# Layer 1's row terms by way of VectorE and DRAM, and a new pace for the dense jobs at the end, in a two-layer graph-attention kernel on Trainium2

## The chip, the cores and the metric

One core of a Trainium2 chip runs the whole program. The metric is the device time of one execution in microseconds (us). TensorE is called PE (matmuls) and PEld (its weight loads), VectorE DVE, ScalarE ACT, GpSimd POOL, and SyncE SP. SP does no arithmetic here: it issues most of the DMA transfers, in the order in which the program lists them. POOL issues the indirect transfers (gathers and scatters of rows by an index).

## The reference, cut to what matters

The input is 64 batches of 256 nodes with 256 features, all in float32, and one adjacency matrix. There are two layers, each a graph attention followed by a feed-forward part, with a layernorm before each and a residual behind each. Layer 0 has four heads and a dense feed-forward. Layer 1 is the one that the change touches:

```python
h = jnp.matmul(inp, W)                       # inp = layernorm(x)
e_src = jnp.einsum('bnf,f->bn', h, a1)
e_dst = jnp.einsum('bnf,f->bn', h, a2)
e = leaky_relu(e_src[:, :, None] + e_dst[:, None, :], 0.01)
attention = softmax(where(adj == 0, -1e9, e))
x = x + relu(matmul(attention, h))
# then, for every token, the two best of 8 experts:
h = gelu(tokens @ w1[e] + b1[e]); y = h @ w2[e] + b2[e]
out = out + combine[:, e:e + 1] * y
```

The score matrix `e` needs one term along the rows and one along the columns. The kernel holds one of them per partition. The other has to appear along the free dimension, the same in all 128 partitions: these are the "row terms" of the title.

## The kernel before, in words

**Steps and ranks.** The whole program is put in order by a planner at the end of the kernel (L1240 to L1282). Each job is a Python generator. A batch begins every three steps (`TICKS = 3`). In a step the planner resumes all active jobs in the order of their rank. `yield 45` ends a job's part of this step and gives its rank in the next one; `yield -26` asks to be resumed within the same step, at rank 26. So the order of instructions on every engine and on every DMA queue is the order of steps and ranks.

**One batch** (`batch_layers`) goes through some 20 steps. Of layer 0: rank 22 projects (L469), rank 24 scales on DVE (L485) and turns the four heads' row terms with a 32x32 block transpose into `ut` (L537). Rank 31 of the same step writes `ut` to a scratch tensor in DRAM (L621), rank 52 reads it back into all 128 partitions of `z` (L554, 512 KB). These two transfers are on SP's queue from batch 18 on (`SETTLED` is 18). The scores (L570) follow two steps later and read the terms from `z` itself.

Of layer 1: twelve steps after the batch's start `projected1` runs at rank 20. PE multiplies (L504), and ACT makes the exponentials `ex` (L511), the scaled `q` (L512) and the mask times one term, `me` (L517). One step later, at rank 25, `scores1` (L520) lets PE transpose the column `ex[:, t, 1:2]`, repeated over 128 columns, into the PSUM tile `pd` (L523, two transposes per batch). DVE then makes the scores `z1` from `pd` (L528, two instructions per batch). One step later, at rank 40, `attended` multiplies them with `q` (L584).

Because a batch starts every three steps, layer 1's `projected1` of batch b shares its step with layer 0's projection of batch b + 3.

**Experts.** The first 61 batches (`ROUTED`) are routed: POOL sends every token's row to its two experts' regions in DRAM (L1066), and whole pairs of 128-row tiles are worked on by `expert_pair`. It loads rows and weights (L906, L917, L935), turns the rows (L117), and some steps later runs `hidden` (L968 and the gelu L974), then `result` (L983, L993) and the weighting (L961). Then `scatter` adds the two tiles to the output with two indirect transfers (L1004). Each of the two waits for both transfers of the pair before. There are 129 pairs. From step 165 on (`SINGLE_AT`) at most one pair begins per step. The tile `y` that a scatter reads has nine buffers.

The last three batches are not routed. Each of 8 experts is applied to all their rows (`dense_expert`: L968, L983, L1036): a first group of batch 61 alone, and a second of batches 62 and 63. These sixteen jobs wait in `dense_jobs` and are begun by the planner. The next one begins once as many steps have gone by as the last one has batches:

```python
            if dense_jobs and step >= dense_free:
                units, job = dense_jobs.pop(0)
                dense_free = step + units
                begin(job(), 90)
```

Of the kernel before, what the change touches and what calls it, by code (L numbers as in the profile page):

```python
# [9 lines left out]
F32 = mybir.dt.float32  # L10
I32 = mybir.dt.int32
AF = mybir.ActivationFunctionType
ALU = mybir.AluOpType
AX = mybir.AxisListType

P = 128
# [5 lines left out]
def rows_to_all(ap: bass.AP, n: int) -> bass.AP:  # L22

    return bass.AP(tensor=ap.tensor, offset=ap.offset, ap=[[0, P], [1, n]])
# [3 lines left out]
def kernel(  # L28
# [17 lines left out]
    nc = tc.nc  # L46
    B, N, D = x.shape
# [4 lines left out]
    NT = N // P  # L52
# [21 lines left out]
    work = ctx.enter_context(tc.tile_pool(name="work", bufs=2))  # L74
    small = ctx.enter_context(tc.tile_pool(name="small", bufs=4))
# [3 lines left out]
    def bank(name, shape):  # L79
        t = psum.tile([P, 2 * D], F32, tag="bank", name=name, bufs=8)  # L80
        n = 1
        for s in shape:
            n *= s
        t = t[:, :n]
        if len(shape) == 2:
            t = t.rearrange("p (a b) -> p a b", a=shape[0])
        elif len(shape) == 3:
            t = t.rearrange("p (a b c) -> p a b c", a=shape[0], b=shape[1])
        return t
# [22 lines left out]
    S = 32  # L112
    G = P // S
# [15 lines left out]
    SETTLED = CHUNKS[0] + CHUNKS[1] + CHUNKS[2] + CHUNKS[3] + 2  # L129


    ident = const.tile([P, P], F32, tag="ident", name="ident")
# [186 lines left out]
    def once(work):  # L319
# [14 lines left out]
        out=tri, in_=tri, pattern=[[1, P]], base=0, channel_multiplier=-1,  # L334
# [64 lines left out]
    def finish_norms(n):  # L399
        mv, rstd = half_done.pop()  # L400
        if at_end():
            var = small.tile([P, 2 * NT], F32, tag="sq", name="var", bufs=4)[:, :n]
            nc.vector.tensor_scalar(var, mv[:, :n, 1], EPS, None, op0=ALU.add)
            inverse_root(rstd[:, :n], var)
            return
        nc.gpsimd.tensor_scalar_add(rstd[:, :n], mv[:, :n, 1], EPS)  # L406
        nc.gpsimd.tensor_tensor(rstd[:, :n], rstd[:, :n], mhalf[:, :n], ALU.pow)
# [84 lines left out]
    for i in range(2):  # L492
        t = keep.tile([P, NT, D + 1], F32, tag=f"q1_{i}", name=f"q1_{i}")
# [3 lines left out]
    def projected1(xT, rstd, b):  # L497

        q = q1s[b % 2]
        pqs = []  # L500
        for t in range(NT):
            pq = bank("pq", [D + 3])
            for k in range(KT):
                nc.tensor.matmul(  # L504
                    pq, xT[:, k, t * P : (t + 1) * P], wx1[:, k, :],
                    start=(k == 0), stop=(k == KT - 1),
                )
            pqs.append(pq)
        ex = small.tile([P, NT, 3], F32, tag="ex1", name="ex1")
        for t, pq in enumerate(pqs):  # L510
            nc.scalar.activation(ex[:, t, :], pq[:, D:], AF.Exp, scale=rstd[:, t : t + 1])  # L511
            nc.scalar.activation(  # L512
                q[:, t, :D], pq[:, :D], AF.Copy, scale=rstd[:, t : t + 1]
            )
        me = work.tile([P, NT, N], F32, tag="me", name="me", bufs=1)
        for j in range(NT):
            nc.scalar.activation(me[:, j, :], masks[1][:, j, :], AF.Copy, scale=ex[:, j, 0:1])  # L517
        return q, ex, me

    def scores1(ex, me):  # L520
        pd = bank("pd", [N])
        for t in range(NT):
            nc.tensor.transpose(  # L523
                pd[:, t * P : (t + 1) * P], ex[:, t, 1:2].to_broadcast([P, P]), ident
            )
        z = work.tile([P, NT, N], F32, tag="z1", name="z1", bufs=1)
        for j in range(NT):
            nc.vector.scalar_tensor_tensor(  # L528
                z[:, j, :], pd, ex[:, j, 2:3], me[:, j, :], op0=ALU.max, op1=ALU.mult
            )  # L530
        return [z[:, j, :] for j in range(NT)]

    def send_terms(q, b):


        ut = small.tile([P, S], F32, tag="ut", name="ut", bufs=1)
        nc.vector.transpose(  # L537
            ut.rearrange("p (t h w) -> p t h w", t=NT, h=H), q[:, :, :, HD - 1 : HD + 3]
        )
        ud = tc.dram_tile([S, S], F32, name=f"terms_{b}")  # L540
        ud = ud.rearrange("c r -> (c r)").rearrange("(c p) -> c p", p=P)
        return ut, ud
# [51 lines left out]
    def batch_layers(b, c0, xng, lg):  # L594
# [23 lines left out]
        if b:  # L618
            ut, ud = send_terms(q, b)
            yield -31  # L620
            terms_queue(b).dma_start(  # L621
                out=ud.rearrange("c (g r) -> g c r", g=G),
                in_=ut[2 : P : S // (NT * H), :],
            )
            yield -52
        z = work.tile([P, NT, NT, H, P], F32, tag="z4", name="z4", bufs=2)
# [17 lines left out]
        ex = work.tile([P, NT, D], F32, tag="e", name="e", bufs=1)  # L644
# [21 lines left out]
        for t in range(NT):  # L666
            nc.vector.scalar_tensor_tensor(  # L667
                x2[:, t, :], pf[:, t, :], rstd[:, t : t + 1], x1b[:, t, :],
                op0=ALU.mult, op1=ALU.add, accum_out=sums[:, t : t + 1],
# [6 lines left out]
        xT = transposed(x2)  # L676
        yield 20
        q, ex, me = projected1(xT, rstd, b)
        yield 25
        z = scores1(ex, me)  # L680
        yield 40
        pvs, rinv = attended(
            q[:, :, None, :], 1, lambda j, h, t: z[j][:, t * P : (t + 1) * P]
# [9 lines left out]
        for t in range(NT):  # L693
            nc.vector.scalar_tensor_tensor(
                x2[:, t, :], x2[:, t, :], 1.0, rel[:, t, :],
                op0=ALU.mult, op1=ALU.add, accum_out=sums[:, t : t + 1],
# [36 lines left out]
        if not dense:  # L733
            d = nc.sync.dma_start(
                out=out_rows[b * N : (b + 1) * N, :].rearrange("(t p) d -> p t d", p=P), in_=base
# [262 lines left out]
    def scatter():  # L998

        y, xt = scatters.pop(0)  # L1000
        before = added[-2:] + based
        based.clear()
        for t in range(2):
            d = nc.gpsimd.indirect_dma_start(  # L1004
                out=out_rows, out_offset=bass.IndirectOffsetOnAxis(
                    ap=xt[:, t, 0:1].bitcast(I32), axis=0
                ),
                in_=y[:, t, :], in_offset=None, compute_op=ALU.add,
            )
            nc.gpsimd.nop()  # L1010
            tc.declare_no_dep(
                d.ins, query=SYNC, group="out", keep=before,
                reason="the rows of a pair are all different",
            )
            for ins in before:
                tc.add_manual_dep(d.ins, ins.name, AFTER, reason="added to before")
            tc.add_to_no_dep_group("out", d.ins)
            added.append(d.ins)
# [37 lines left out]
    active = []  # L1056
    waiting, dense_jobs = [], []
    sent = []

    def begin(job, rank):  # L1060
        active.append([rank, len(order), job])
        order.append(job)
# [172 lines left out]
    step, more, credit = 2, True, 0.0  # L1235


    SETUP_AT = 4
    dense_free = 0
    with tc.manual_schedule():  # L1240
        while more or active or waiting or dense_jobs or scatters:
            phase = step % TICKS
            if more and (phase == 0 or step == 2):
                nxt = next(batches, None)
                more = nxt is not None
                if more:
                    begin(nxt, 40 if phase == 0 else 25)
            if step >= SETUP_AT and setup:
                begin(setup.pop(0)(), 90)
            if step >= SINGLE_AT:  # L1250
                if waiting and len(scatters) < 3:
                    begin(waiting.pop(0)(), 90)
            elif phase == 1:
                credit = min(credit + 3.0, 2.0)
                while waiting and credit >= 1.0:
                    credit -= 1.0
                    begin(waiting.pop(0)(), 90)
            if dense_jobs and step >= dense_free:
                units, job = dense_jobs.pop(0)
                dense_free = step + units  # L1260
                begin(job(), 90)
            if scatters:
                def one():
                    scatter()
                    return
                    yield
                begin(one(), 97)
            order_steps.append(step)
            queue = [(a[0], a[1], a) for a in active]
            heapq.heapify(queue)  # L1270
            while queue:
                *_, entry = heapq.heappop(queue)
                entry[0] = next(entry[2], None)
                if entry[0] is not None and entry[0] < 0:
                    entry[0] = -entry[0]
                    heapq.heappush(queue, (entry[0], entry[1], entry))
            if half_done:
                finish_norms(NT)
            if half_squared:
                finish_squares()  # L1280
            active[:] = [a for a in active if a[0] is not None]
            step += 1  # L1282
# [35 lines left out]
```

## Time and profile before

| | before |
|---|---|
| median of 3 runs | 1486.76 us (1486.30 to 1491.11) |
| profiled execution, its own time | 1489.83 us |
| span from first to last instruction | 1488.0 us |
| PE busy, PEld busy | 1420.1 us (95%), 1264.0 us (85%) |
| DVE busy | 1232.9 us (83%) |
| ACT busy | 1006.5 us (68%) |
| POOL busy | 864.6 us (58%) |
| moved by DMA | 236.10 MB, mean 159 GB/s |
| granted PE clock, mean | 0.985 |

The shares are averages over a start, a long middle in which two pairs and one batch are done every 20 us, a stretch from about 1050 us with one pair per step, and an end without batches from about 1310 us. A share of a stage is read from that stage alone. The ends of matmuls are modelled, so a busy PE is judged by the starts that follow each other and by the idle time ahead of them.

### The profile page before, as it was taken

How to read it: one execution, taken by the hardware profiler on the slowest of the kernel's cores; microseconds unless marked ns; L12 is line 12 of the kernel's file. 1: busy time of each engine (PE TensorE's matmuls, PEld its weight loads, DVE VectorE, ACT ScalarE, POOL GpSimd, SP SyncE). 2: the span in 40 equal slices, each digit the busy share in tenths (PEclk: the TensorE clock that was granted, in tenths of full speed). 3: DMA queues.
4: the chain of work that ended last, by engine and by line, in shares of the span. 5: the costliest groups of instructions: out<-in, count | busy, mean ns of one | idle time of the engine just before them, and what ended most of it. 6: DMA issues, size and time to landing. Idle time of an engine off the chain costs nothing. (4 is left out here: it accounts for less than half of the span.)

```text
span 1488.0 us, 29865 instructions
## 1 busy us (share of the span) xinstructions
PE 1420.1 (95%) x8138; PEld 1264.0 (85%) x8138; DVE 1232.9 (83%) x4320; ACT 1006.5 (68%) x2389; POOL 864.6 (58%) x851
## 2 busy tenths in 40 slices
PE   6899999999999999999999999999999999899994
PEld 5688888898999999899999989888888888778883
DVE  7689999988898889899888989998888888765442
ACT  1377667577777777777777787777777878643330
POOL 2122446455857676666758585776666668544444
PEclk9899999999999999999999999999999999999998
DMA  4832243567878777787877687768877786988743
GB/s 128 227 98 86 89 130 117 146 172 153 199 171 193 161 177 170 171 185 180 190 156 190 147 193 168 190 164 186 193 158 172 153 173 128 213 201 150 152 66 49
DMA packets 354081, 236.10 MB, mean 159 GB/s; under 512 B 246260, under 2 KB 316156, under 8 KB 353916
## 3 DMA queue, kind: packets, MB, share of 16 engines
q1 hardware_dynamic: 301000, 157.90, 42.1%
q0 software_dynamic: 48864, 66.33, 23.9%
q10 hardware_dynamic: 4052, 9.98, 2.3%
q8 instruction: 67, 1.10, 0.3%
q14 instruction: 98, 0.80, 0.2%
HBM read 146.00 MB, written 88.09 MB: 157 GB/s over the span
## 5 line engine op out<-in xcount | busy, mean ns | idle before, releaser
L1004 POOL DMA_INDIRECT out_dram<-y,xt x258 | 415.6, 1611 | 214.6 <-issue 54.6
L584 PE MATMUL pv<-q,z 128*128 128x65 f32 (+1 forms) x2560 | 363.7, 297 | 0.7 <-DVE z L570 0.3
L584 PEld LDWEIGHTS pv<-q,z 128*128 128x128 f32 x2560 | 331.2, 193 | 13.3 <-DVE z L570 1.3
L1066 POOL DMA_INDIRECT xs<-xng,pos x244 | 256.3, 1050 | 65.2 <-issue 57.7
L983 PE MATMUL py<-w2s,hT 128*128 (+1 forms) x1224 | 282.9, 382 | 4.7 <-ACT hT L974 4.5
L983 PEld LDWEIGHTS py<-w2s,hT 128*128 128x128 f32 x1224 | 229.7, 191 | 37.2 <-ACT hT L974 7.4
L570 DVE SCALAR_TENSOR_TENSOR z<-z,q,mask 128x256 f32<-128x256 f32 x504 | 231.5, 482 | 15.5 <-DMA z<-terms 6.5
L968 PE MATMUL ph<-sT,we 128*128 128x256 f32 x1032 | 241.4, 383 | 1.6 <-DVE sT L117 0.9
L968 PEld LDWEIGHTS ph<-sT,we 128*128 128x128 f32 x1032 | 195.6, 192 | 28.7 <-DVE sT L117 1.4
L961 ACT ACTIVATE y<-y,w 128x256 f32<-128x256 f32 x258 | 113.4, 499 | 119.4 <-DVE y L993 119.2
L459 ACT COPY xT<-pt 128x512 f32<-128x512 f32 x209 | 121.2, 588 | 82.1 <-PE pt L453 80.0
L974 ACT ACTIVATE hT<-ph,we 128x256 f32<-128x256 f32 x306 | 124.1, 472 | 64.1 <-PE ph L968 46.7
L406 POOL TENSOR_SCALAR rstd<-mv 128x4 f32<-128x4 f32 (+1 forms) x66 | 15.9, 240 | 224.8 <-DVE mv L379 175.3
L504 PE MATMUL pq<-wx,xT 128*128 128x259 f32 x512 | 126.5, 390 | 13.9 <-ACT xT L459 13.9
L424 ACT ACTIVATE off<-x,sums 128x256 f32<-128x256 f32 x256 | 129.2, 505 | 9.2 <-DVE x L667 3.3
L993 DVE TENSOR_TENSOR y<-py,b2s 128x512 f32<-128x512 f32 x129 | 86.9, 687 | 56.3 <-PE py L983 44.8
L469 PE MATMUL pq<-wx,xT 128*128 128x268 f32 x512 | 128.1, 394 | 2.4 <-DVE xT L117 1.2
L504 PEld LDWEIGHTS pq<-wx,xT 128*128 128x128 f32 x512 | 96.0, 192 | 33.6 <-ACT xT L459 19.8
L660 PE MATMUL pf<-wfT,xT 128*128 128x256 f32 x512 | 124.2, 386 | 0.0
L469 PEld LDWEIGHTS pq<-wx,xT 128*128 128x128 f32 x512 | 97.9, 192 | 21.7 <-DVE xT L117 1.4
L688 ACT ACTIVATE rel<-pv,rinv 128x256 f32<-128x256 f32 x128 | 54.0, 469 | 82.1 <-DVE rinv L591 81.8
L660 PEld LDWEIGHTS pf<-wfT,xT 128*128 128x128 f32 x512 | 94.9, 196 | 10.6
(170 smaller groups left out, 2355.7 us busy)
## 6 DMA issues: line engine op xcount, KB each, us to landing
we<-wpack SPq DMA_DIRECT2D x145, 288.0 KB
xr<-xs SPq DMA_DIRECT2D x516, 64.0 KB
z<-terms SPq DMA_DIRECT2D x46, 512.0 KB
xin<-in_x_dram SPq DMA_DIRECT2D x64, 256.0 KB
out_dram<-base SPq DMA_DIRECT2D x61, 256.0 KB
xblk<-in_x_dram SPq DMA_DIRECT2D x188, 64.0 KB
z<-terms ACTq DMA_DIRECT2D x17, 512.0 KB
out_dram<-y,xt POOLq DMA_INDIRECT x258
```

Source lines behind the costliest of these rows:

```text
L424: nc.scalar.activation(off, src[:, t, :], AF.Square, bias=sums[:, t : t + 1], scale=-float(D), accum_out=sq[:, at + t : at + t + 1],)
L459: nc.scalar.copy(dst, pt)
L469: nc.tensor.matmul(pq.rearrange("p h c -> p (h c)"), xT[:, k, t * P : (t + 1) * P], wx[:, k, :], start=(k == 0), stop=(k == KT - 1),)
L504: nc.tensor.matmul(pq, xT[:, k, t * P : (t + 1) * P], wx1[:, k, :], start=(k == 0), stop=(k == KT - 1),)
L570: nc.vector.scalar_tensor_tensor(z[:, j, :, h, :], terms, q[:, j, h, HD + 2 : HD + 3], masks[0][:, j, :].rearrange("p (t i) -> p t i", t=N ...
L584: nc.tensor.matmul(pv[:, h, :], z(j, h, t), q[:, j, h, : d + 1], start=(j == 0), stop=(j == NT - 1),)
L660: nc.tensor.matmul(pf[:, t, :], xT[:, k, t * P : (t + 1) * P], wfT[:, k, :], start=(k == 0), stop=(k == KT - 1),)
L968: nc.tensor.matmul(ph[:, f, :], we[:, k * D + f * P : k * D + (f + 1) * P], xT[:, k, :], start=(k == 0), stop=(k == KT - 1),)
L974: nc.scalar.activation(hT[:, f, :], ph[:, f, :], AF.Gelu, bias=we[:, C_B1 + f : C_B1 + f + 1])
L983: nc.tensor.matmul(py[:, t, :], hT[:, f, t * P : (t + 1) * P], w2s[:, e, f * D : (f + 1) * D].rearrange("p e c -> p (e c)"), start=(f == 0 ...
L1004: d = nc.gpsimd.indirect_dma_start(out=out_rows, out_offset=bass.IndirectOffsetOnAxis(ap=xt[:, t, 0:1].bitcast(I32), axis=0), in_=y[:, t, ...
L1066: d = nc.gpsimd.indirect_dma_start(out=xs_d[: E * CAP * PAIR, :], out_offset=bass.IndirectOffsetOnAxis(ap=at, axis=0), in_=xe, in_offset=None,
```

## The change

From batch 18 on, layer 1's row terms take the way that layer 0's terms take. In the step of `projected1`, at rank 26, DVE turns the column into `ut1` (`turned_terms1`). At rank 31 SP writes 256 floats to DRAM, and at rank 52 it reads them back into all 128 partitions of the second half of `z1` (128 KB). `scores1` then runs in the next step, as before, but at rank 45 instead of 25, and takes the terms from `z1` instead of `pd`. For the first 18 batches the transposes by PE stay.

The planner's `dense_free` becomes a fraction. As long as a pair waits or runs, a dense job is given 1.25 steps per batch of its group, and after that 0.5.

```diff
+    def turned_terms1(ex, b):
+        ut = small.tile([P, S], F32, tag="ut1", name="ut1", bufs=1)
+        nc.vector.transpose(
+            ut.rearrange("p (t w) -> p t w", t=NT),
+            ex[:, :, 1:2].to_broadcast([P, NT, S // NT]),
+        )
+        return ut, tc.dram_tile([N], F32, name=f"terms1_{b}")
+
+    def scores1(ex, me, z, spread):
+        terms = z[:, NT - 1, :]
+        if not spread:
+            terms = bank("pd", [N])
+            for t in range(NT):
+                nc.tensor.transpose(
+                    terms[:, t * P : (t + 1) * P], ex[:, t, 1:2].to_broadcast([P, P]), ident
+                )
         for j in range(NT):
             nc.vector.scalar_tensor_tensor(
-                z[:, j, :], pd, ex[:, j, 2:3], me[:, j, :], op0=ALU.max, op1=ALU.mult
+                z[:, j, :], terms, ex[:, j, 2:3], me[:, j, :], op0=ALU.max, op1=ALU.mult
             )
...
         q, ex, me = projected1(xT, rstd, b)
-        yield 25
-        z = scores1(ex, me)
+        spread = b >= SETTLED
+        if spread:
+            yield -26
+            ut, ud = turned_terms1(ex, b)
+            yield -31
+            nc.sync.dma_start(
+                out=ud.rearrange("(t g r) -> g t r", t=NT, g=G),
+                in_=ut[0 : P : S // NT, :],
+            )
+            yield -52
+        z = work.tile([P, NT, N], F32, tag="z1", name="z1", bufs=1)
+        if spread:
+            nc.sync.dma_start(out=z[:, NT - 1, :], in_=rows_to_all(ud, N))
+        yield 45 if spread else 25
+        z = scores1(ex, me, z, spread)
         yield 40
...
-    dense_free = 0
+    dense_free = 0.0
...
                 units, job = dense_jobs.pop(0)
-                dense_free = step + units
+                pairs = waiting or any(a[2].__name__ == "expert_pair" for a in active)
+                dense_free = max(dense_free, step - 0.5) + units * (1.25 if pairs else 0.5)
                 begin(job(), 90)
```

More of the change, by code (lines that the diff above doesn't have):

```diff
@@ L518, in projected1 @@
         return q, ex, me
[L520 to L526, printed above, removed]
+    def turned_terms1(ex, b):
[13 more added lines that the diff above has]
+                )
         for j in range(NT):
             nc.vector.scalar_tensor_tensor(
-                z[:, j, :], pd, ex[:, j, 2:3], me[:, j, :], op0=ALU.max, op1=ALU.mult
+                z[:, j, :], terms, ex[:, j, 2:3], me[:, j, :], op0=ALU.max, op1=ALU.mult
             )
```

## The prediction

> **What bounds the kernel now.** I read the stages first (busy time by windows), then the groups of instructions by shape, then the timeline of one step, then the waits of SP's queue, and last the timeline of the end. The first view has one row per stretch, with busy us and count for each engine.
>
> ```profile
> core 0: us, PE busy (x) PEld busy (x) DVE busy (x) ACT busy (x) POOL busy (x), PEclk, DMA share, GB/s
> 530.00:610.00 80.00, 80.00 (x478) 72.48 (x477) 71.49 (x245) 61.49 (x146) 54.58 (x52) 1.00 0.78 176
> 1050.00:1210.00 160.00, 155.74 (x879) 137.53 (x878) 137.57 (x487) 126.93 (x276) 108.39 (x98) 1.00 0.80 173
> 1310.00:1440.00 130.00, 127.70 (x594) 111.98 (x595) 69.76 (x187) 52.33 (x123) 57.78 (x38) 1.00 0.75 143
> ```
>
> From 370 to 930 us every stretch looks like the first row: four batches take exactly 80 us, and PE has no idle time at all. There, what PE no longer does is won, so long as nothing else comes to 20 us per batch. DVE is nearest: 71.5 of 80 us, some 3 us of small gaps between instructions, and 5.3 us of waiting (2.2 for ACT at L485, 1.9 for PE at L667, 1.1 at L993).
>
> The operations concerned, in the groups by shape (busy us, mean ns of one):
>
> ```profile
> L523 PE MATMUL pd<-ident,ex 128*128 128x128 f32 x128 | 26.2, 278 | 2.0 <-ACT ex L511 1.9
> L528 DVE SCALAR_TENSOR_TENSOR z<-pd,ex,me 128x256 f32<-128x256 f32 x128 | 53.8, 460 | 0.0
> L570 DVE SCALAR_TENSOR_TENSOR z<-z,q,mask 128x256 f32<-128x256 f32 x504 | 231.5, 482 | 15.5 <-DMA z<-terms 6.5
> L537 DVE STREAM_TRANSPOSE ut<-q 128x32 f32<-128x32 f32 x63 | 13.4, 212 | 2.2
> ```
>
> The 278 ns of a transpose is a latency. What it costs PE is the distance between starts:
>
> ```profile
> 810.93 0.38 PE L523 MATMUL pd<-ident,ex 128*128 128x128 f32 x2
> ...
> 811.15 3.68 PE L584 MATMUL pv<-q,z 128*128 128x65 f32 x32
> ```
>
> 811.15 - 810.93 = 0.22 us for both, and 0.218 in nearly every batch.
>
> The end has another limit. In this timeline the ACT row makes one pair's `y` ready at 1428.68; counted from the last, it belongs to the scatter at 1457.56:
>
> ```profile
> 1427.77 0.91 ACT L961 ACTIVATE y<-y,w 128x256 f32<-128x256 f32 x2 [1.61 <-DVE y L993]
> ...
> 1451.12 1.56 POOL L1004 DMA_INDIRECT out_dram<-y,xt  x1 [3.08 <-ACT hT L974]
> 1452.98 1.56 POOL L1004 DMA_INDIRECT out_dram<-y,xt  x1 [0.30 <-issue]
> 1457.56 1.56 POOL L1004 DMA_INDIRECT out_dram<-y,xt  x1 [3.02 <-DMA out_dram<-y,xt]
> ```
>
> The scatter comes 29 us after its `y`, and behind the landing of the scatter before (the "ACT hT" on another row cannot be it, since `y` was long there). Scatters follow each other at 6.4 us, which is two issues, the gap and 3 us of landing. Lining up all 129, I find the lag growing from 15 us at pair 105 to 33 us. So from about 1310 us a chain of some 23 scatters sets the end, 7.5 us each while pairs' rows are still loaded (to 1403 us) and 6.4 us after, though PE is busy there too.
>
> [...] SP issues layer 0's write L621 at 809.22 and its read L554 waits for that write to land; in half the batches the read is issued 1.72 us after the write, in the others up to 3.1. [...] The trace has 482 ns for the SBUF form (L570) and 460 for the PSUM form, so I take no gain.
>
> ```profile
> SPq L621 <- DVE stats L378: 321.8, 45, 11.9
> SPq L554 <- DMA terms<-ut: 49.5, 46, 2.3
> ```
>
> (Total us, times, longest.) SP stands 7 us per batch waiting for `ut`, so it has time to spare.
>
> **The change, part by part.**
>
> *PE loses* two transposes in each of the batches 18 to 63: 46 x 0.218 = 10.0 us. Counting also the waits for ACT ahead of some late ones (up to 0.56 us each), 11.9 is the most.
>
> *DVE gains* one 32x32 transpose: 0.21 us and a gap of 0.04, so 0.25 per batch, 11.6 in all. L528 may go from 414 (its fastest) to 482 ns, at most 0.13 per batch[...].
>
> *The wait* that takes the place of `pd`: `ut1` follows layer 0's `ut` on DVE. I add up the way to `z1` with each batch's own times for layer 0: 0.03 from DVE to SP's issue, 1.7 to 3.1 to the read's issue, 1.0 to 2.0 to its first packet, then an estimated 0.9 for 8 packets of 1 KB on each of 16 engines (0.1 us each in the trace) and 0.4 for the semaphore (the write's last packet ends 1.32 after its issue, SP goes on at 1.72). That makes 4.3 to 5.7, mean 4.9 us. The window, from `ut` to L528, is 4.2 to 5.4 us up to batch 51 and 3.4 to 4.2 in most batches after. The rank 45 changes little, since no other job has DVE work between 25 and 45 in that step. Batch by batch DVE waits 0 to 0.5 us up to batch 49, and 0.4 to 1.8 from 50 to 60, 16 us in all. Behind the waiting L528 stand the normalisation of layer 0's attention, `x2` (L667) and the turning of rows (L117). Does it reach PE? The free part of DVE's time in the middle is 5.3/4 = 1.3 us per batch; less 0.25, 0.13 and the 0.22 by which PE's batch gets shorter, 0.7 is left against a mean wait of 0.15. After 1050 us DVE waits 2.3 us per batch, and 1.7 is left against 1.2. Directly, PE's first matmul on `z1` comes 8.8 to 15.9 us after `ut`, and 4.9 + 0.9 is needed. The cover is thin only in the last batches, where a step has little work. I take a loss of 1 us, with 0 and 4 as bounds.
>
> *SP* issues two more transfers, some 0.5 and 0.35 us. Layer 1's write goes ahead of layer 0's (its job is older at rank 31), and its read ahead of layer 0's read, so the 512 KB come about 0.8 us later. Their scores are two steps later; the row loads behind slide by 0.8 us into SP's 7 us. *POOL's* queue is not passed. *DMA* gains 46 x 128 KB, 5.9 of 236 MB: nothing.
>
> *The dense jobs.* Following the yields step by step: before, 19 of the 24 batch-and-expert units have their `hidden` ahead of the last pair's `result`, after the change 15. Each costs PE 3.45 us, so the last `y` is ready 4 x 3.45 = 13.8 us sooner. But scatters already lag 31 us; now they lag 44.5. That is 44.5/6.45 = 6.9 pairs, and `y` has nine buffers, so nothing stalls and nothing is won. Row loads end two units, 7 us, sooner: one pair at 6.4 instead of 7.5 us, 1 us won (0 to 3). Behind the last pair's `result`, 1432 instead of 1446 us on the old clock, nine units are left instead of five: four in sequence at 4.3 us (the spacing from 1447 us on), two steps with two side by side at an estimated 7.3 and a last one at 4.3, 36 us and some 2 to finish. That ends dense PE work near 1470 us, as before (1469.3), so its stores land some 10 us ahead of the last scatter. I book 0 for the whole part.
>
> Sum: -10.0 + 1 + 0 = -9 us, which the scatter chain takes over because its start moves with PE. The profiled execution (1489.83) would become 1480.8. The median lies 3.07 below it: **1477.8 us**, likely 1474 to 1482.
>
> **The rivals.**
>
> *The round trip binds DVE* (slower). In the middle a batch gets longer by the trip, less the mean window of 4.9 us, the 0.7 of free time and the 0.22 that PE wins. So it turns at a mean trip of 5.8 us, and every us over that costs 46 us. At 6.5 us: +32, so 1519; at 6.0, +9, so 1496. For it: DMA is 78% busy, and some trips of layer 0 reach 5.7. Against: the read is the first behind the write, and four times smaller than layer 0's. Chance 0.08.
>
> *The end gives it back.* From 1050 us POOL's scatters run at 8.2 us per pair, little over their own pace with rows loading. If they set the time from there, the late 12 batches (2.6 us) count for nothing, and DVE's late waits add up to 3: about -4, so 1483. Against it is a lag that stays at 18 us there. Chance 0.12.
>
> *The end shrinks.* If loads that end sooner free not one but six scatters of the 1.1 us, it is -15, so 1472. Against: the same bytes are only packed closer. Chance 0.15.
>
> *It does not do what it says*: if the planner's test for running pairs were never true, dense jobs would come at full pace, and the chain would end the same: -9 again, no case of its own.
>
> **How the numbers follow.** The forecast has 0.65, and the rivals 0.08, 0.12 and 0.15. What a measurement of this kernel can tell is about 0.3%, 4.5 us. Faster: most of the forecast and the last rival, with some of the second, 0.82. Same: the second's rest and the forecast's weak edge, 0.10. Slower: 0.08. The range reaches from 1470 (the shrinking end) to 1484 (the gain given back).
>
> **What would show it.** In the changed profile, the transposes into `pd` are 36 instead of 128; the transpose `ut1` appears 46 times at 0.2 us; four batches in the middle take 79.1 us with PE still not idle; L528 waits for a DMA, under 0.5 us in the middle and some 1 us late; scatters follow each other at 6.4 to 7.5 us to the end, with a lag over 40 us; dense PE work ends ahead of them. It is wrong if PE shows idle time behind DVE in the middle, if the wait ahead of L528 is over 1.5 us there, or if the last thing to end is not a scatter.

## The result, and the profile after

| | before | after |
|---|---|---|
| median | 1488.88 us (6 runs) | 1552.2 us (6 runs, 1547.23 to 1558.71) |
| profiled execution, span | 1488.0 us | 1545.5 us |
| ratio of the times | | 1.0425 [1.0395, 1.0454] |

The change costs 63 us. The prediction was 1477.8 with 1484 as its upper end, so its direction was wrong. What came is the rival to which it gave 0.08: the round trip binds DVE.

Busy time by windows, the same stretches as shown of before (the last row now reaches back into the batches, since layer 1 of batch 63 starts only at 1328.8 us):

```profile
530.00:610.00 80.00, 75.95 (x445) 67.94 (x444) 69.60 (x237) 58.48 (x139) 53.95 (x51) 1.00 0.75 172
1050.00:1210.00 160.00, 147.50 (x803) 129.10 (x802) 127.55 (x459) 114.09 (x248) 95.79 (x87) 0.97 0.76 166
1310.00:1440.00 130.00, 121.54 (x561) 104.03 (x561) 84.02 (x347) 66.42 (x160) 63.77 (x49) 0.97 0.87 184
```

In the middle PE was busy for all of 80 us; now it idles for 4 of them, and DVE is not busier but less busy (69.6 instead of 71.5). Every engine's share falls, so what got longer is waiting. The groups by shape name the wait (busy us, mean ns | idle before them, and what ended it):

```profile
L539 DVE SCALAR_TENSOR_TENSOR z<-z,ex,me 128x256 f32<-128x256 f32 x92 | 44.6, 485 | 69.4 <-DMA z<-terms 67.5
L523 DVE STREAM_TRANSPOSE ut<-ex 128x32 f32<-128x32 f32 x46 | 7.9, 171 | 0.9 <-ACT ex L511 0.9
L535 PE MATMUL pd<-ident,ex 128*128 128x128 f32 x36 | 7.8, 282 | 1.7 <-ACT ex L511 1.7
```

The counts are as the change says: 36 transposes into `pd` are left, 46 turns on DVE, 92 score instructions from `z1`. The idle time ahead of those 92 is new: 67.5 us for the read of the terms. The list of waits shows where it spreads to:

```profile
ACT e L656 <- DVE hp L650: 88.7, 46, 5.7
...
DVE z L539 <- DMA z<-terms: 67.5, 45, 3.4
...
PEld pq L504 <- ACT xT L459: 59.9, 42, 3.5
```

Before, ACT waited 22.6 us for `hp`, and PE's weight load 19.8 us for `xT`:

```profile
ACT e L645 <- DVE hp L639: 22.6, 31, 3.1
```

One step in the timeline shows the first half of the way, `hp` being layer 0's attention, normalised on DVE right behind the scores:

```profile
621.61 0.17 DVE L523 STREAM_TRANSPOSE ut<-ex 128x32 f32<-128x32 f32 x1
621.80 0.58 SPq L695 DMA_DIRECT2D terms<-ut  x1
622.44 0.51 SPq L632 DMA_DIRECT2D terms<-ut  x1
622.99 0.45 SPq L96 DMA_DIRECT2D xin<-in_x_dram  x1
623.55 0.40 SPq L702 DMA_DIRECT2D z<-terms  x1
...
628.34 1.00 DVE L539 SCALAR_TENSOR_TENSOR z<-z,ex,me 128x256 f32<-128x256 f32 x2 [2.18 <-DMA z<-terms]
...
629.47 0.76 DVE L650 TENSOR_TENSOR hp<-pv,rinv 128x256 f32<-128x256 f32 x2
...
630.26 0.63 ACT L656 ACTIVATE e<-hp 128x512 f32<-128x512 f32 x1 [2.71 <-DVE hp L650]
```

The scores begin 628.34 - 621.78 = 6.56 us behind the turn. Between write and read on SP stands a line that the prediction overlooked: L96, the load of a later batch's input, 256 KB, has rank 40 and so goes ahead of the read at rank 52. It stood between layer 0's write and read in before, too:

```profile
809.81 0.45 SPq L96 DMA_DIRECT2D xin<-in_x_dram  x1
812.00 0.35 SPq L554 DMA_DIRECT2D z<-terms  x1
```

There it was issued 2.19 us ahead of the read (1.15 us in the median of batches 18 to 48), here 0.56 us. On ACT, behind `e`, come the sums of a layernorm, the gelus and then the copy of `xT`, and PE's next projection waits for that (636.04 and 636.69 us in this step, PE idle 1.56 us).

By stages, from the starts of `projected1` (L504) in both profiles: batch 18 to 48 takes 630.5 us instead of 600.6 (+29.9), batch 48 to 63 377.1 instead of 353.6 (+23.5), and from there to the end 216.6 instead of 210.6 (+6.0). The missing -2.0 lies ahead of batch 18; the sum is the 57.4 us between the two spans.

### The profile page after: what moved, and what is told of

The parts are those of the page before. It is cut to its first block, busy times and chain, and to the rows that moved or that the text cites. A ratio compares the mean times of both kernels' runs of the same rounds, so it can differ in the third digit from the quotient of the medians.

```text
span 1545.5 us, 29834 instructions
## 1 busy us (share of the span) xinstructions
PE 1432.9 (93%) x8046; PEld 1265.2 (82%) x8046; DVE 1243.1 (80%) x4366; ACT 1006.7 (65%) x2389; POOL 870.1 (56%) x851
## 5 line engine op out<-in xcount | busy, mean ns | idle before, releaser
L595 PEld LDWEIGHTS pv<-q,z 128*128 128x128 f32 x2560 | 335.5, 194 | 14.6 <-DVE z L581 0.7
L504 PE MATMUL pq<-wx,xT 128*128 128x259 f32 x512 | 134.2, 407 | 45.5 <-ACT xT L459 45.4
L504 PEld LDWEIGHTS pq<-wx,xT 128*128 128x128 f32 x512 | 97.5, 198 | 73.9 <-ACT xT L459 59.9
L469 PEld LDWEIGHTS pq<-wx,xT 128*128 128x128 f32 x512 | 99.7, 195 | 22.1 <-DVE wx L168 1.3
L656 ACT ACTIVATE e<-hp 128x512 f32<-128x512 f32 x64 | 40.4, 631 | 111.4 <-DVE hp L650 88.7
L453 PE MATMUL pt<-ident,x 128*128 128x128 f32 x512 | 85.0, 283 | 21.0 <-DVE x L678 21.0
```

The source lines that it names most:

```text
L469: nc.tensor.matmul(pq.rearrange("p h c -> p (h c)"), xT[:, k, t * P : (t + 1) * P], wx[:, k, :], start=(k == 0), stop=(k == KT - 1),)
L504: nc.tensor.matmul(pq, xT[:, k, t * P : (t + 1) * P], wx1[:, k, :], start=(k == 0), stop=(k == KT - 1),)
L595: nc.tensor.matmul(pv[:, h, :], z(j, h, t), q[:, j, h, : d + 1], start=(j == 0), stop=(j == NT - 1),)
```

## The experiments

Each kernel is compared with the kernel before on the same chip: median 1508.08 us on the chip of the first four runs, 1487.4 to 1487.5 on that of the others.

**Which half of the change.** `dense_only` is the kernel before with the two changed lines of the planner; `terms_only` is the kernel after without them.

> The kernel before with the new pace of the dense jobs alone; layer 1's terms still go through PE and pd. Theory A (the terms' way costs it all, and the end is a chain of scatters): within 0.3% of before, since the last y comes some 14 us sooner but the scatters set the end. Theory B (the new pace costs part): slower by 5 us or more, with longer periods of the scatters from pair 104 on, since in the profile of the changed kernel the stretch from scatter 103 to the last took 5.7 us more.

> The changed kernel with the old pace of the dense jobs. Theory A: slower than before by the whole 63 us (58 to 66), with four batches in the middle at 84 us and DVE waiting 1.3 us per batch ahead of the scores. Theory B: 5 us or more better than the changed kernel.

Measured: dense_only 1508.19 us, 0.9999 [0.9975, 1.0024]. terms_only 1551.03 us, 1.0278 [1.0246, 1.0310]. That is a loss of 43 us where 58 to 66 were expected: on this chip the kernel before is 20 us slower, and the changed kernel is not. The stages of terms_only are near those of after (631.0, 382.9 and 208.9 us instead of 630.5, 377.1 and 216.6), and DVE waits 69.0 us for the terms instead of 67.5. So the loss lies in the terms' way.

**Is it the wait?** `late72` lets the scores run at rank 72 instead of 45, at the end of the step: the trip stays, but DVE has other work ahead of the scores.

```diff
-        yield 45 if spread else 25
+        yield 72 if spread else 25
```

> The changed kernel with layer 1's scores at rank 72 instead of 45 of the same step, so that on DVE they stand behind layer 0's normalisation hp and behind x2, with the same work on every engine. Theory A1 (a loop: the wait ahead of the scores delays hp, ACT's e waits for hp ahead of the gelus and of the copy xT, and PE's projection waits for xT): the idle time of PE ahead of the projection goes, four batches take 79 to 80 us, and the time is 1476 to 1490. Theory A2 (DVE has too much to do, wherever it stands): most of the loss stays, over 1520.

Measured: 1508.5 us, 0.9997 [0.9981, 1.0013]. The wait of L539 is down to 0.2 us in all (in the profiled execution, which with 1499.26 us was the fastest of 22), and with it the whole loss is gone. So the work that the change adds to DVE, SP and the DMA engines costs next to nothing by itself on this chip: 1508.5 us against 1508.08. That the gain on PE did not appear was a miss of my expectation.

**What makes the trip long?** `xin_later` is the kernel after with the load L96 issued one step later, so that it no longer stands between write and read.

> The changed kernel with the load of the next batch's rows (256 KB, SP's queue) issued one step later, so that it no longer stands ahead of the read of layer 1's terms. If the read is slow because it queues behind those packets: from issue to the scores about 3.2 us instead of 4.4, the wait on DVE falls from 1.3 to 0.3 us or less, and the time to 1490 to 1510. If it is slow because of layer 0's 512 KB read behind it, or by itself: 4.2 us or more as before, and the time stays over 1535.

Measured: 1527.45 us, 1.0125 [1.0091, 1.0159]. On SP's queue the read now follows the two writes:

```profile
629.03 0.54 SPq L697 DMA_DIRECT2D terms<-ut  x1
629.62 0.51 SPq L634 DMA_DIRECT2D terms<-ut  x1
631.60 0.35 SPq L704 DMA_DIRECT2D z<-terms  x1
```

and DVE's wait is less:

```profile
DVE z L539 <- DMA z<-terms: 42.1, 41, 2.8
```

In batches 18 to 48, from the read's issue to the start of the scores it is 3.6 us, against 4.3 in terms_only on the same chip and 4.4 in after. The packets tell why, if they are told apart by the order in which they start. In after, 256 packets of 1 KB of the load start ahead of the read's 128, whose first starts 1.7 us after its issue and whose last at 4.0 (means of these batches). Here the first starts at 1.0, and the last at 3.1. The load's place is thus worth 0.7 us of the trip and, from batch 18 to 48, 16.7 us of time (614.3 us instead of 631.0 in terms_only). Neither expectation was met: the wait fell to 0.64 us, not to 0.3, and the time lies between the two. Most of what is still lost lies behind batch 48 (375.1 us to batch 63, 362.2 in dense_only), where DVE waits 1.7 us per batch up to batch 60. And 6.0 us of the gain over terms_only lie ahead of batch 18, where no batch takes the new way yet, so not all of it can be put down to the trip.

**Does the place of the wait matter, or DVE's time?** I suspected the first: the wait stands ahead of `hp`, and `hp` leads to PE. Two kernels put the same delay, four idle multiplications of 128x128 on DVE per batch from 18 on, into the kernel before: ahead of the scores, and behind `hp` and `x2`.

```diff
+    def delay(n):
+        for _ in range(n):
+            nc.vector.tensor_tensor(mean_w, mean_w, ones, ALU.mult)
...
+        if b >= SETTLED:
+            delay(4)
         z = scores1(ex, me)
```

> The kernel before, with four extra multiplications of 128x128 on DVE (some 0.3 us each, 1.3 us in all, about the wait that the change brought) ahead of layer 1's scores from batch 18 on. No DMA is added and the terms still go through pd. Theory A1 (loop: what delays hp delays ACT's e, the gelus and the copy xT behind it in ACT's order, and PE's projection): 0.7 to 1.2 us per batch, slower by 32 to 55 us, with PE idle ahead of the projection. Theory A2 (only the sum of DVE's work counts): DVE comes to 79.9 of 80 us per four batches, so 0 to 10 us, and the same as with the delay elsewhere.

> The same four multiplications in the same step, but at rank 72, behind hp and x2 on DVE. Theory A1: they delay neither hp nor x2, so the cost is under 12 us, a third or less of the other place. Theory A2: the same cost as ahead of the scores, within 8 us.

Measured: 1512.21 us, 1.0173 [1.0142, 1.0204] ahead of the scores, and 1520.18 us, 1.0204 [1.0175, 1.0233] behind. That the place decides is refuted: the delay behind `hp` costs as much or more (batches 18 to 48 take 617.9 and 617.1 us). That DVE has time for it is refuted as well. What costs is DVE's time, in either place. The waits of DVE from 450 to 930 us (total us, times, longest) show what could be filled. Before:

```profile
DVE q L485 <- ACT q L477: 12.7, 23, 0.6
DVE x L667 <- PE pf L660: 11.5, 18, 0.8
DVE y L993 <- PE pd L523: 5.8, 6, 1.0
```

With the delay ahead of the scores:

```profile
DVE q L489 <- ACT q L481: 12.9, 24, 0.6
DVE y L999 <- PE pd L527: 5.6, 6, 1.0
```

The delay has eaten the wait at `x2` (L667) and left the two others as they were. These 480 us hold 24 batches of 20 us, so here it could fill 11.5/24 = 0.48 us per batch, and not the 1.3 us that all three waits add up to.

`delay_half` (two multiplications) asks whether there is such a threshold.

> The kernel before with two idle VectorE instructions of 0.28 us (with their gaps 0.65 us) ahead of the layer-1 scores from batch 18 on, half of delay_before_scores (which had 1.3 us per batch and lost 24.8 us, 20.0 to 20.6 us per batch in the middle). Theory D1 (a threshold: VectorE needs 18.6 us per batch with its small gaps, another 0.7 us of its waits can't be filled, so 0.7 us per batch are free and only what goes beyond lengthens the batch): the middle stays at 20.0 to 20.1 us per batch, and the whole loses 0 to 5 us, most of it after batch 49: 1.000 to 1.0035. Theory D2 (no threshold, each us on VectorE costs about 0.45): 20.3 us per batch, +12 us, 1.008.

Measured: 1492.85 us, 1.0033 [1.0018, 1.0049]. Batches 18 to 48 take 601.9/30 = 20.06 us each in its profile, so here the threshold holds and the proportional rule fails; the loss comes after batch 48 (359.5 instead of 353.6 us to batch 63). Its row from 530 to 610 us against that of the full delay, first the half and then the full one:

```profile
530.00:610.00 80.00, 80.00 (x477) 72.19 (x475) 72.71 (x250) 60.89 (x145) 54.25 (x51) 1.00 0.76 174
```

```profile
530.00:610.00 80.00, 78.95 (x469) 70.86 (x468) 73.01 (x255) 60.12 (x142) 53.36 (x51) 1.00 0.73 168
```

With half the delay PE still has no idle time; with all of it DVE stands at 73 of 80 us and PE loses one, with no wait for a DMA. That is not the most that DVE can do in 80 us: `early_late`, below, has 73.82 and a PE that is never idle.

**Where is PE's gain?** `early` turns at rank 21, writes at 23 and reads at 39, ahead of the 256 KB load; the scores stay at rank 45. `early_late` also puts the scores at rank 72.

```diff
-            yield -26
+            yield -21
             ut, ud = turned_terms1(ex, b)
-            yield -31
+            yield -23
...
-            yield -52
+            yield -39
```

> The changed kernel with the way to z1 begun sooner and kept clear: ut1 at rank 21 (on DVE ahead of layer 0's scaling, some 1.7 us sooner), its write at 23, and its read at 39, ahead of the load of 256 KB at rank 40. The scores stay at 45. If the trip is late for where its two transfers stand in the queues: the read's data lands before DVE comes to the scores, the mean wait is under 0.15 us, and the time is 4 to 12 us under the kernel before (46 x 0.218 us of PE). If the trip is slow by itself (4.3 us from the read's issue, as in the changed kernel): a wait of 0.5 us or more stays, and it is slower than before by 5 to 25 us.

> Both: the way begun sooner, and the scores at rank 72, behind hp and x2. hp no longer waits for the scores either, so the loop gets shorter by their 0.9 us. If PE is then the only bound: 8 to 12 us under the kernel before, at most 3 better than the early way alone. If something else holds the time (the moved scores made no gain over before although PE does less): within 4 us of the kernel before.

Measured: early 1496.29 us, 1.0056 [1.0033, 1.0078]; early_late 1489.24 us, 1.0009 [0.9996, 1.0021]. In early, DVE waits 0.09 us per batch for the terms up to batch 48 and 0.42 from 49 to 60. So neither expectation holds whole: the wait went as in the first, and the time, 9 us over before, is that of the second. For early_late the second holds. early_late from 530 to 610 us:

```profile
530.00:610.00 80.00, 80.00 (x478) 72.62 (x477) 73.82 (x253) 62.41 (x148) 55.15 (x55) 1.00 0.78 184
```

PE is without idle time again. Batches 18 to 48 take 594.3 us instead of 600.6: 6.3/30 = 0.21 us per batch. The predicted gain of PE is real, and shows as soon as DVE doesn't wait. In DVE's waits from 450 to 930 us L485, which both delays left alone, is gone from the list; the turn, which now stands ahead of it, waits instead, and for less than half as long:

```profile
DVE ut L523 <- ACT ex L511: 5.5, 19, 0.3
```

So a wait that work in one place leaves as it is can get shorter when work stands in another. But from batch 48 on the gain is given back, 573.7 us to the last instruction instead of 564.2.

By what? The 2x2 of the next three runs with early_late changes the dense pace back (`dense_before`), and lets the new way end with batch 48 (`mid`):

```diff
-        spread = b >= SETTLED
+        spread = SETTLED <= b < 49
```

> The kernel of early_late with the planner's pace for dense jobs as before. In early_late the middle took 0.21 us per batch less than before (6.3 us ahead of before at batch 48), but was 4.3 ahead at batch 63 and behind at the end. Theory C1 (the new dense pace gives the gain back behind the last batch): ratio 0.997, some 4 us faster than the kernel before. Theory C2 (the gain is lost from batch 49 on, and the dense pace costs nothing): 0.999 to 1.002, as early_late.

> The kernel of early_late, but only batches 18 to 48 go by VectorE and DRAM; from 49 on TensorE transposes as before. The dense pace is the new one. C1: the 31 batches win 31 x 0.21 = 6.5 us, the dense pace takes some 4 of it: 0.998. C2: all of the 6.5 us stay: 0.9955. A third theory C3 (from 1050 us the scatter chain on GpSimd sets the time whatever TensorE wins before): 0.999 to 1.001, because what is won ahead of it is lost to waiting there.

> Batches 18 to 48 by VectorE and DRAM with the early ranks and the scores at rank 72, TensorE's transposes from 49 on, and the dense pace as before. C1 and C2 both: 6.5 us faster than before, 0.9955. C3: 0.999 to 1.001.

| ratio to before | new dense pace | dense pace as before |
|---|---|---|
| new way for 18 to 63 | 1.0009 [0.9996, 1.0021] | 0.9999 [0.9980, 1.0017] |
| new way for 18 to 48 | 0.9991 [0.9976, 1.0006] | 0.9983 [0.9969, 0.9997] |

The last one, 1484.58 us, is the only version that beats both kernels, the one before by 3 us, and only just more than nothing. The intervals of neighbours overlap, so neither step is shown alone; the point values would give 2.4 to 2.7 us to the late batches and 1.2 to 1.5 to the pace. Of the 6.3 us that the middle wins, half does not arrive even there. In its profile, against that of before, 2.4 of them are lost behind batch 48 (355.6 instead of 353.6 us to batch 63, 211.0 instead of 210.6 from there to the end). None of C1, C2 and C3 gives these numbers, and by what they are lost stays open.

## Why the prediction was wrong, point by point

**PE loses 10 us of work**: right. 0.218 us per batch was read from the starts, and 0.21 is what the middle gains once nothing else binds it (early_late).

**DVE's added work**: right. 0.171 us and a gap for the turn, 485 ns for the scores from SBUF. In the middle DVE's busy time per batch goes from 17.9 to 69.03/80 x 21.02 = 18.14 us (mean of the six rows from 450 to 930), 0.25 more. The scores from SBUF are the dearer ones here, 485 ns against 466 for the 36 that still read `pd`.

**The trip**: the first term that failed. Up to batch 48, write to read was 1.73 us, the low end of what I took. Read to scores was 4.44 us where I had added up 2.3 to 3.3. The term that was mis-sized is my estimate of 0.9 us for eight packets on each of 16 engines (an even split, which no trace here shows): the first and the last start 2.3 us apart, and 2.1 even without the load (xin_later). I had worked it out from the packets' durations alone, 0.1 us each. That is what packets of 1 KB take on GpSimd's queue (102 ns in the median of before); on SP's they take 46 ns, so eight of them last 0.37 us, and their duration is not what sets the 2.3. Layer 0's own read in before could have told: 128 packets of 172 ns (median), so 1.4 us by the same sum, and 3.3 us from the first start to the last. The first packet came at 1.7 us, inside the range that I took, but later than the mean of layer 0's (1.2); for that 0.5 us, what else SP issues between ranks 31 and 52 (the 256 KB of L96) was not looked at. It is made up for by the read's issue, which came 0.4 us sooner than layer 0's mean of 2.15. So the trip was 6.2 us and not 4.9, and DVE waited 1.33 us per batch and not 0.15.

**DVE's free time**: the second term that failed, and the one that the rival shared. I counted every wait of DVE as time that other work can fill, 1.3 us per batch, and had 0.7 left after the additions. The delays show that, for work at the scores or behind `x2`, only the wait at L667 is, 0.48 us. The rule that comes out for this kernel is: a batch takes PE's time, or 20.0 us plus what is added to DVE there beyond 0.48, whichever is more. From profiles, batches 18 to 48 (a delay counts from its first instruction to the scores):

| kernel | added to DVE per batch, us | by the rule, us | measured, us |
|---|---|---|---|
| delay_half | 0.49 | 20.0 | 20.06 |
| delay_before_scores | 1.15 | 20.7 | 20.60 |
| after | 0.25 + wait 1.33 | 21.1 | 21.02 |
| early | 0.25 + wait 0.09 | 19.8 (PE) | 19.87 |

So wait and work count alike. The rule is not tried on the chip of the first four runs, where the middle of the kernel before is itself longer (20.38 us per batch in dense_only); late72 takes 20.04 there, with 0.25 added and no wait, and the rule would give 19.8. For the trip of 6.2 us the rival's formula, with 0.7 us free, gave 46 x 0.4 = 18 us; with the free time as found the rule gives 1.1 us for each of the first 31 batches. The late ones lose 23.5/15 = 1.6 each; DVE waits 1.9 us for the terms there (batches 49 to 60), and a step has less other work. With that wait at 0.42 (early) batches 48 to 63 take 363.0 us instead of 377.1, and without it (early_late) 356.6, so most of their loss goes with the wait, too. Why the two other waits of DVE don't shrink under the delays is not shown. One waits for ACT's `q`, which comes from PE's projection in the same step, and it may move along with a longer batch, which is a guess; early_late, with work ahead of it, has less of it.

**"Does it reach PE?"**: I compared means of free time and wait, and asked only when PE needs `z1` itself. The longer way, `hp`, `e`, gelu, `xT`, next projection, was not followed. That the loss goes by this way alone is not shown, since a delay behind `hp` costs as much. In before its last link has little slack: in one step `xT` is ready at 802.97 and PE starts on it at 803.27.

**SP**: two issues of 0.58 and 0.40 us, near the 0.5 and 0.35 costed; that they slide others was small, but that others slide them was not looked at.

**The dense jobs**: right as far as told apart. No measurable cost or gain in the kernel before (dense_only). The end ran as described: the last `y` was ready at 1489.2 us, and its scatter came 46.5 us later (44.5 predicted), behind a chain at 6.4 us:

```profile
1522.20 1.58 POOL L1028 DMA_INDIRECT out_dram<-y,xt  x1 [3.00 <-DMA out_dram<-y,xt]
1524.08 1.56 POOL L1028 DMA_INDIRECT out_dram<-y,xt  x1 [0.30 <-issue]
1528.57 1.55 POOL L1028 DMA_INDIRECT out_dram<-y,xt  x1 [2.93 <-DMA out_dram<-y,xt]
```

DVE's last dense work ends at 1526.58, ahead of the last scatter at 1537.55. "Which the scatter chain takes over because its start moves with PE" held for the loss, which arrived whole, but not for the gain: early_mid_dense_before keeps half.

## What to carry to other kernels

Here a wait on DVE, busy for 71.5 of 80 us before, cost what work of the same length costs: 1.33 us of wait and 0.25 of work made a batch 21.02 us long, 1.15 us of work alone 20.60. Ask which of an engine's present waits are real slack for work in the place in question, by adding idle work there in two doses and seeing which waits shrink, before counting their sum as free: of 1.3 us only 0.48 were. Look at what is issued on the same queue between the write and the read of a round trip over DRAM: the 256 KB load that stood there, with its packets ahead of the read's, was worth 0.7 of 6.2 us. And look up how far apart the first and the last packet of another read of the kernel start: layer 0's 128 packets took 3.3 us where their durations add up to 1.4, and those of the new read 2.3 where I had 0.9. Moving the user of the read to the end of the step took the whole cost away here, and beginning the trip sooner, with the read ahead of a large load, all but 9 us; taking 0.21 us per batch off the busiest engine, 6.3 us from batch 18 to 48, was then worth 3 us (early_mid_dense_before).

## What the runs showed of the hardware that was not expected

- A 128 KB read in 1 KB packets behind a 256 KB load of 1 KB packets on the same queue: first packet 1.7 us after its issue (after) instead of 1.0 (xin_later, with the load elsewhere), though the load was issued only 0.56 us earlier.
- Its 128 packets take 46 ns each (median), but the first and the last of all start 2.1 us apart (xin_later) to 2.3 us (after). What lies between them was not followed.
- On the chip of the first four runs the kernel before is 20 us slower. dense_only shows a wait there that the trace of before, from elsewhere, has not among its main ones; its cause is open:

```profile
DVE rinv L591 <- PE pt L453: 29.3, 24, 2.7
```
